# A selective-scan network on one core: the remainder of delta in a tile of its own, and delta * u on GpSimd

## The chip, the cores and the metric

The kernel runs on one core of one Trainium2 chip. The metric is the device time of one execution in microseconds. Three runs of the kernel before took 11978.79, 11985.35 and 12007.12 us; the median is 11985.35 us. One further execution was profiled.

Five engines appear below: TensorE (PE in the profile, its weight loads PEld), VectorE (DVE), ScalarE (ACT), GpSimd (POOL) and SyncE (SP), which issues all DMA transfers of this kernel from one queue. [...]

## The reference

The network has four layers on an input of 4 images of 64 x 64 pixels with 96 channels. Layers 0 and 1 are two-dimensional selective scans (a residual connection around each), layers 2 and 3 are attention and a feed-forward network with quantised weights. The change lies in layers 0 and 1. Cut to what matters:

```python
xz = einsum('bhwc,ec->bhwe', groupnorm(x), in_proj_w)       # 2 * E channels, E = 192
xx, z = split(xz, 2);  z = silu(z)
xc = silu(depthwise_conv3x3(xx) + conv_b)
xs = [xc by rows, xc by columns, both reversed]             # K = 4 directions, L = 4096 steps
dts, Bmat, Cmat = split(einsum('bkdl,kcd->bkcl', xs, x_proj_weight), [R, R + N])
delta = softplus(einsum('bkrl,kdr->bkdl', dts, dt_projs_weight) + dt_projs_bias)
# scan over L, with A = -exp(A_logs), N = 16 states per channel
h = exp(delta * A) * h + delta * B * u                      # u = xs
y = sum over n of h * C
out = out_proj(layernorm(sum of the 4 directions of (y + u * D)) * z)
```

Two quantities made from delta are needed for the scan: delta itself, for the decay exp(delta * A), and the product delta * u.

## The kernel before, in words

`run` goes through four phases: layer 0 with images 0 and 1, layer 0 with images 2 and 3, then layer 1 with the same two pairs. A phase has a preparation (`prepare`), a scan (`scan_phase`) and a finish (`finish`). The finish of one phase is interleaved with the preparation of the next: both are Python generators, `run` steps the finish a certain number of times for each step of the preparation (`ph.beside`). After the last finish `token_layers` computes layers 2 and 3.

**The preparation.** Statistics of the group norm come first, then the convolution of the first image (`convolve`), then the loop over images i, chunks c of 512 positions and directions k = 0 (by rows) and 1 (by columns), which calls `steps`. After each call of `steps` for the first image, two steps of the convolution of the second image are taken. So a preparation has three stretches: convolution alone; items of the first image with the convolution of the second ("convolution stage" below); and items of the second image alone ("tail"). In phases two to four the finish of the phase before runs beside all of them.

A convolution tap is one VectorE instruction on two SBUF operands, xp and xc (L268), eight of them per 512 positions, after a first one on ScalarE.

**`steps`.** One call handles direction k and its reverse, k + 2: two "items". TensorE makes dts, B and C of both (L291, tile c in PSUM); ScalarE adds a row of ones and copies to SBUF (L294, L295, tile xd); TensorE multiplies by the weights of delta (L308, tile d, two buffers in PSUM). Then for each of the two items:

- L316, ScalarE: delta = softplus(d), tile dl, 96 partitions x 1024 fp32 (two halves of 512 positions)
- L317, ScalarE: the first part, delta rounded to bf16, into parts[:, 0]
- L318, VectorE: du = delta * u, tile du_sb; u is a view of xc. For k = 0 its elements are adjacent (in either direction), for k = 1 they are 64 floats apart
- L319, VectorE: delta - first part, written over dl
- L321, SP: du goes to DRAM, twice (two copies, 384 KB each)
- L322, GpSimd: the second part, the rest rounded to bf16
- L323, VectorE: the third part, rest - second part, rounded to bf16
- L324, SP: the three parts go to DRAM (576 KB)

Delta is thus kept as three bf16 numbers whose sum is delta, so that the scan can spread it over partitions with one bf16 matrix product (L415). The tiles dl, parts and du_sb come from the pool "steps" with two buffers each: the third use of a tile waits until every reader of the first is done, du_sb and parts until their transfers have landed. There are 64 items in a phase and 256 in all.

**The order of the work.** In the preparation and the finish a list scheduler of the tile framework decides the order of the instructions on each engine from its own cost estimates, and sets the semaphore waits. In the scan the order is written out by hand.

**The scan.** A unit is 12 channels of one chunk for all 8 sequences and 16 states. Its tile h is filled with du by DMA (L399), multiplied by B on GpSimd (L409), scanned on VectorE (L426) with a decay that TensorE and ScalarE make (L415, L419), and contracted with C on TensorE (L444). The scan's tiles are allocated when the pools of the preparation have been released.

Of the kernel before, what the change touches and what calls it, by code (L numbers as in the profile page):

```python
# [9 lines left out]
F32 = mybir.dt.float32  # L10
# [4 lines left out]
ALU = mybir.AluOpType  # L15
# [7 lines left out]
C = 96  # L23
# [6 lines left out]
TC = 512  # L30
# [25 lines left out]
def scan_view(t, k, c):  # L56


    part, half = t.ap[0], t.ap[1]
    if k == 0:  # L60
        off, steps = TC * c, (HW, 1)
    elif k == 1:
        off, steps = ROWS * c, (1, HW)
    elif k == 2:
        off, steps = L - 1 - TC * c, (-HW, -1)
    else:
        off, steps = L - 1 - ROWS * c, (-1, -HW)
    return bass.AP(t.tensor, t.offset + off, [part, half, [steps[0], ROWS], [steps[1], HW]])


def view(t, off, *dims):

    return bass.AP(t.tensor, t.offset + off, [t.ap[0]] + [list(d) for d in dims])


def rows(t):

    if len(t.shape) == 2:
        return t.rearrange("p (r w) -> p r w", w=HW)
    return t.rearrange("p h (r w) -> p h r w", w=HW)  # L80
# [50 lines left out]
class Scans:  # L131
# [152 lines left out]
    def steps(self, ph, sp, xc, xp, dt_w, i, k, c):  # L284


        nc, cst = self.nc, self.cst
        u = scan_view(xc, k, c)
        ps = self.bank()
        for h in range(2):  # L290
            nc.tensor.matmul(rows(ps[:XD2]), xp[:, k, h], u[:, h], start=h == 0, stop=h == 1)  # L291
        xd = sp.tile([XD2, TC], F32, name="xd")

        nc.scalar.activation(xd[:XD], ps[:XD], AF.Identity, bias=cst.one_row[:XD])  # L294
        nc.scalar.activation(  # L295
            xd[64:], view(ps[64:XD2], TC - 1, (-1, TC)), AF.Identity, bias=cst.one_row[64:]
        )
        yield
        both = []
        for back in range(2):  # L300
            at = 64 * back
            g, cc = 2 * (k + 2 * back) + i, NC - 1 - c if back else c
            nc.sync.dma_start(ph.bc[cc][:, g], xd[at : at + 2 * NS])
            both.append((g, cc, scan_view(xc, k + 2 * back, cc), self.p_d.tile([C, 2, TC], F32, name="d")))
        for m in range(2):
            for back, (_, _, _, ps) in enumerate(both):
                part = slice(64 * back + 2 * NS, 64 * back + XD)
                nc.tensor.matmul(  # L308
                    ps[:, m], dt_w[part, k, m * C : (m + 1) * C], xd[part], start=True, stop=True
                )  # L310
        yield
        for g, cc, u, ps in both:
            delta = sp.tile([C, 2, TC], F32, name="dl")
            parts = sp.tile([C, NP16, 2, TC], BF16, name="parts")
            du = sp.tile([C, 2, TC], F32, name="du_sb")
            nc.scalar.activation(delta, ps, AF.Softplus)  # L316
            nc.scalar.copy(parts[:, 0], delta)  # L317
            nc.vector.tensor_tensor(rows(du), rows(delta), u, ALU.mult)  # L318
            nc.vector.tensor_tensor(delta, delta, parts[:, 0], ALU.subtract)  # L319
            for copy in range(2):  # L320
                nc.sync.dma_start(ph.du[cc][copy, g, :E].rearrange("(h e) t -> e h t", h=2), du)  # L321
            nc.gpsimd.tensor_copy(parts[:, 1], delta)  # L322
            nc.vector.tensor_tensor(parts[:, 2], delta, parts[:, 1], ALU.subtract)  # L323
            nc.sync.dma_start(  # L324
                ph.delta[cc][g].rearrange("n (h q) t -> q (n h) t", h=2),
                parts.rearrange("q n h t -> q (n h) t"),
            )
            yield
# [660 lines left out]
```

## Time and profile before

| what | value |
|---|---|
| median of three runs | 11985.35 us |
| the profiled execution | 11973.68 us, span 11971.9 us |
| granted TensorE clock, mean | 0.826 |
| VectorE busy | 10052.3 us (84%) |
| of it scans, L426 | 6345.7 + 868.3 us |
| of it products du, L318 | 416.2 us in 256 instructions |
| of it differences, L319 and L323 | 309.6 and 329.1 us |
| of it convolution taps, L268 | 713.8 us in 1024 instructions |
| GpSimd busy | 7465.3 us (62%) |
| of it h * B, L409 | 7021.1 us in 2048 instructions |
| of it casts, L322 | 416.1 us in 256 instructions |
| ScalarE busy | 7321.2 us (61%) |
| preparations (from the first statistics, or the last scan instruction, to the loads of the next scan) | 12 to 712, 2598 to 3450, 5320 to 6166, 8034 to 8886 us |
| first and last VectorE scan instruction of each scan | 737 to 2598, 3474 to 5320, 6192 to 8034, 8910 to 10768 us |

How to read it: "busy" is the time in which an engine has an instruction of this program under way. An instruction that is blocked after it began counts as busy for the whole time. A line of a group names source line, engine, operation, what it writes and reads with partitions x elements, the count, busy time and mean duration, then the idle time of the engine just before these instructions and what ended it. A line of the timeline gives start and duration in us, and in brackets the idle time of the engine before it and what ended that. A line of the waits names who waited for whom, the sum in us, how often, and the longest. A line of the busy times by stage gives, after the stretch and its length, the busy time and count of each engine, the granted TensorE clock, the busy share of the DMA engines, and their rate.

### The profile page before, as it was taken

What the parts mean: (1) busy time and instruction counts of PE and PEld (TensorE: products, weight loads), DVE (VectorE), ACT (ScalarE), POOL (GpSimd) and SP (SyncE); (2) the same over time, 40 slices, a digit from 0 to 9 for tenths busy, and PEclk for the clock granted to TensorE, in tenths of its full rate; (3) what the DMA queues carried; (4) which work ended last, traced back from release to release, by engine and by line L of the source; (5) the groups of instructions that cost most, each with busy time, mean ns of one, the idle gap of its engine ahead of it and who ended that gap; (6) DMA issues with size and microseconds to landing.
All of it is one profiled execution on the core that took longest, in us unless ns stands there. A gap on an engine that the chain in (4) does not pass through costs nothing.

```text
span 11971.9 us, 337755 instructions
## 1 busy us (share of the span) xinstructions
PE 8659.6 (72%) x144960; PEld 4597.6 (38%) x144960; DVE 10052.3 (84%) x10351; ACT 7321.2 (61%) x12109; POOL 7465.3 (62%) x2316
## 2 busy tenths in 40 slices
PE   3567777765767777765777777766677777777777
PEld 1124444442334444442334444433234444444333
DVE  6679999987769999987769999986769999993667
ACT  4556666655556666655556666654557666662556
POOL 0169999960149999970149999970139999990000
PEclk8579999986679989886679999986668999998887
DMA  3677777764677777765677777764677777763110
GB/s 98 185 244 254 255 252 252 252 206 138 197 231 255 254 256 257 257 216 143 193 226 256 258 257 252 258 219 136 199 221 258 255 254 250 254 232 125 18 21 11
DMA packets 952267, 2501.23 MB, mean 209 GB/s; under 512 B 324494, under 2 KB 607220, under 8 KB 819316
## 3 DMA queue, kind: packets, MB, share of 16 engines
q1 hardware_dynamic: 950772, 2479.63, 62.8%
q8 instruction: 1142, 18.71, 0.7%
q14 instruction: 353, 2.89, 0.1%
HBM read 1965.42 MB, written 513.80 MB: 207 GB/s over the span
## 4 chain that ended last, share of the span: by engine, by line
DMA 56%; PE 12%; DVE 11%; SPq 10%; ACT 5%; issue 4%; POOL 2%; POOLq 0%; DVEq 0%; ACTq 0%
DMA h<-du 52%; SPq L399 9%; DVE xc L268 4%; PE f L594 2%; POOL parts L322 2%; PE d L308 1%; PE c L291 1%; DVE parts L323 1%; DVE dl L319 1%; DVE du_sb L318 1%; DMA yk<-y 1%; PE c L251 1%; PE f L603 1%; PE f L674 1%; PE f L660 1%
## 5 line engine op out<-in xcount | busy, mean ns | idle before, releaser
L409 POOL TENSOR_TENSOR h<-h,b 128x1536 f32<-128x1536 f32 x2048 | 7021.1, 3461 | 533.5 <-DMA h<-du 191.9
L426 DVE TENSOR_TENSOR_SCAN h<-a,carry,h 128x512 f32<-128x512 f32 x5376 | 6345.7, 1259 | 174.6 <-POOL h L409 171.9
L419 ACT ACTIVATE a<-a,a_col 128x512 f32<-128x512 f32 x6144 | 4031.0, 664 | 1856.7 <-PE a L415 1830.9
L444 PEld LDWEIGHTS y<-h,cw 128*32 128x32 f32 x131072 | 2786.7, 128 | 3501.2 <-issue 1310.9
L444 PE MATMUL y<-h,cw 128*32 128x48 f32 x131072 | 3660.1, 266 | 527.3 <-DVE h L426 211.6
L415 PE MATMUL a<-dlt,rep 72*128 72x512 bf16 x6144 | 2526.8, 422 | 1302.3 <-DVE h L426 1212.9
L322 POOL CAST parts<-dl 96x1024 bf16<-96x1024 f32 x256 | 416.1, 1630 | 2793.0 <-DVE dl L319 2587.0
L456 ACT COPY d<-y 128x384 f32<-128x384 f32 x2048 | 979.8, 478 | 475.0 <-PE y L444 429.8
L426 DVE TENSOR_TENSOR_SCAN h<-a,h 128x512 f32<-128x512 f32 x768 | 868.3, 1200 | 165.5 <-ACT a L419 142.6
L415 PEld LDWEIGHTS <-rep 72*128 72x128 bf16 x6144 | 487.2, 98 | 829.0 <-issue 587.8
L308 PE MATMUL d<-xd,dt_w 7*96 7x512 f32 x1024 | 631.7, 905 | 237.5 <-ACT dl L316 149.6
L268 DVE SCALAR_TENSOR_TENSOR xc<-xp,conv_w,xc 96x512 f32<-96x512 f32 x1024 | 713.8, 756 | 54.8 <-ACT xc L266 38.9
L826 POOL MEMSET tn<- 1x4096 f32 x8 | 27.8, 3507 | 862.3 <-PE pa L846 515.1
L316 ACT ACTIVATE dl<-d 96x1024 f32<-96x1024 f32 x256 | 258.4, 1018 | 449.5 <-DVE parts L323 429.1
L318 DVE TENSOR_TENSOR du_sb<-dl,xc 96x1024 f32<-96x1024 f32 x256 | 416.2, 1633 | 116.7 <-ACT dl L316 73.0
L291 PE MATMUL c<-xc,x_proj 96*103 96x512 f32 x512 | 452.3, 1024 | 82.1 <-ACT xc L271 42.7
L594 PE MATMUL f<-yk,perm 128*128 128x384 f32 x1024 | 429.6, 564 | 95.4 <-DMA yk<-y 72.8
L251 PE MATMUL c<-rawi,in_w 96*96 96x512 f32 x256 | 206.0, 915 | 397.0 <-DVE rawi L247 312.1
L319 DVE TENSOR_TENSOR dl<-dl,parts 96x1024 f32<-96x1024 f32 x256 | 309.6, 1217 | 210.8 <-ACT parts L317 209.3
L323 DVE TENSOR_TENSOR parts<-dl,parts 96x1024 bf16<-96x1024 f32 x256 | 329.1, 1292 | 160.4 <-POOL parts L322 158.0
L308 PEld LDWEIGHTS d<-xd,dt_w 7*96 7x96 f32 x1024 | 171.8, 222 | 642.9 <-ACT dl L316 229.7
L361 ACT ACTIVATE cw<-c,gmask 128x256 f32<-128x256 f32 x512 | 286.0, 570 | 116.4 <-DMA dlt<-delta 58.1
(116 smaller groups left out, 5802.0 us busy)
## 6 DMA issues: line engine op xcount, KB each, us to landing
h<-du SPq DMA_DIRECT2D x1024, 768.0 KB
h<-du SPq DMA_DIRECT2D x2048, 384.0 KB
du<-du_sb SPq DMA_DIRECT2D x512, 384.0 KB
delta<-parts SPq DMA_DIRECT2D x256, 576.0 KB
dlt<-delta SPq DMA_DIRECT2D x512, 288.0 KB
y<-d SPq DMA_DIRECT2D x2048, 48.0 KB
yk<-y SPq DMA_DIRECT2D x256, 384.0 KB
ud<-xu SPq DMA_DIRECT2D x128, 192.0 KB
```

The source lines that it names most:

```text
L268: nc.vector.scalar_tensor_tensor(rows(acc), src, w, rows(acc), ALU.mult, ALU.add)
L291: nc.tensor.matmul(rows(ps[:XD2]), xp[:, k, h], u[:, h], start=h == 0, stop=h == 1)
L308: nc.tensor.matmul(ps[:, m], dt_w[part, k, m * C : (m + 1) * C], xd[part], start=True, stop=True)
L322: nc.gpsimd.tensor_copy(parts[:, 1], delta)
L399: self.nc.sync.dma_start(u.h[32 * first : 32 * (first + quarters), e : e + n].rearrange("p e t -> p (e t)"), source.rearrange("a g e t -> ...
L409: self.nc.gpsimd.tensor_tensor(h, h, b, ALU.mult)
L415: self.nc.tensor.matmul(u.a[n], self.cst.rep[:, h], u.dl[:, e], start=True, stop=True)
L419: self.nc.scalar.activation(u.a[n], u.a[n], AF.Exp, scale=u.ph.a_col[:, at : at + 1])
L426: self.nc.vector.tensor_tensor_scan(u.h[:, n], u.a.pop(n), u.h[:, n], 0.0 if u.c == 0 else u.ph.carry[:, at : at + 1], ALU.mult, ALU.add,)
L444: self.nc.tensor.matmul(view(u.y[32 * j : 32 * j + 32], l2 * EB, (8 * EB, 4), (1, EB)), u.ph.cw[u.c][:, l1, 8 * j + l2], view(u.h, 64 * l1 ...
L456: self.nc.scalar.copy(u.d[:, :, :, l1], u.y[:, : 32 * EB].rearrange("p (t h x) -> p t h x", t=4, h=2))
L594: nc.tensor.matmul(ps[:, : 4 * C].rearrange("p (w v e) -> p w v e", w=4, v=nv), cst.perm[:, k], view(t, off, (sw if k < 2 else -sw, 4), (1 ...
```

## The change

Two edits in `steps`. The product delta * u is issued on GpSimd instead of VectorE. The difference delta - first part no longer overwrites dl but goes to a new tile "rest", of the same size and from the same pool with two buffers; the second and the third part read it. All other lines are the same, but they stand one line lower from there on (L319 becomes L320, L322 becomes L323, L323 becomes L324, L409 becomes L410 and so on).

```diff
             du = sp.tile([C, 2, TC], F32, name="du_sb")
             nc.scalar.activation(delta, ps, AF.Softplus)
             nc.scalar.copy(parts[:, 0], delta)
-            nc.vector.tensor_tensor(rows(du), rows(delta), u, ALU.mult)
-            nc.vector.tensor_tensor(delta, delta, parts[:, 0], ALU.subtract)
+            nc.gpsimd.tensor_tensor(rows(du), rows(delta), u, ALU.mult)
+            rest = sp.tile([C, 2, TC], F32, name="rest")
+            nc.vector.tensor_tensor(rest, delta, parts[:, 0], ALU.subtract)
             for copy in range(2):
                 nc.sync.dma_start(ph.du[cc][copy, g, :E].rearrange("(h e) t -> e h t", h=2), du)
-            nc.gpsimd.tensor_copy(parts[:, 1], delta)
-            nc.vector.tensor_tensor(parts[:, 2], delta, parts[:, 1], ALU.subtract)
+            nc.gpsimd.tensor_copy(parts[:, 1], rest)
+            nc.vector.tensor_tensor(parts[:, 2], rest, parts[:, 1], ALU.subtract)
             nc.sync.dma_start(
                 ph.delta[cc][g].rearrange("n (h q) t -> q (n h) t", h=2),
                 parts.rearrange("q n h t -> q (n h) t"),
```

## The prediction

> **What bounds the kernel now.** I read the page first, then the busy times by stage, then waits and timeline of the stages that hold the edited lines. The page's busy times suggest a VectorE problem that GpSimd could share:
>
> ```profile
> PE 8659.6 (72%) x144960; PEld 4597.6 (38%) x144960; DVE 10052.3 (84%) x10351; ACT 7321.2 (61%) x12109; POOL 7465.3 (62%) x2316
> L409 POOL TENSOR_TENSOR h<-h,b 128x1536 f32<-128x1536 f32 x2048 | 7021.1, 3461 | 533.5 <-DMA h<-du 191.9
> L318 DVE TENSOR_TENSOR du_sb<-dl,xc 96x1024 f32<-96x1024 f32 x256 | 416.2, 1633 | 116.7 <-ACT dl L316 73.0
> ```
>
> But the 84% is mostly scans (L426), which the change doesn't touch. The edited lines run only in the four preparations (12 to 712, 2598 to 3450, 5320 to 6166 and 8034 to 8886 us), 64 items in each. I cut two preparations where the second convolution starts and where it ends:
>
> ```profile
> core 0: us, PE busy (x) PEld busy (x) DVE busy (x) ACT busy (x) POOL busy (x), PEclk, DMA share, GB/s
> ...
> 230.00:486.00 256.00, 134.45 (x192) 37.85 (x192) 205.65 (x223) 138.66 (x152) 45.82 (x27) 0.53 0.59 165
> 486.00:702.00 216.00, 159.40 (x174) 41.42 (x174) 127.67 (x99) 95.44 (x105) 53.93 (x33) 0.50 0.77 221
> ...
> 2875.00:3143.00 268.00, 180.22 (x363) 70.86 (x364) 222.59 (x283) 160.37 (x185) 46.27 (x26) 0.59 0.63 181
> 3143.00:3425.00 282.00, 234.99 (x617) 112.16 (x615) 176.47 (x233) 144.08 (x181) 43.96 (x31) 0.68 0.72 218
> ```
>
> In the convolution stages VectorE is the fullest engine (206 of 256 us, 223 of 268). In the first preparation's tail no engine is full: there a chain sets the pace, 6.4 us an item. In later tails TensorE is at 235 of 282, because the finish of the previous phase runs beside them.
>
> The timeline of the first tail shows the chain, and something more:
>
> ```profile
> 592.73 1.89 DVE L318 TENSOR_TENSOR du_sb<-dl,xc 96x1024 f32<-96x1024 f32 x1
> 592.92 2.60 POOL L322 CAST parts<-dl 96x1024 bf16<-96x1024 f32 x1 [4.81 <-DVE dl L319]
> 595.56 1.22 DVE L323 TENSOR_TENSOR parts<-dl,parts 96x1024 bf16<-96x1024 f32 x1 [0.94 <-POOL parts L322]
> 596.88 1.02 ACT L316 ACTIVATE dl<-d 96x1024 f32<-96x1024 f32 x1 [5.32 <-DVE parts L323]
> 597.80 1.03 ACT L317 CAST parts<-dl 96x1024 bf16<-96x1024 f32 x1
> 598.86 1.22 DVE L319 TENSOR_TENSOR dl<-dl,parts 96x1024 f32<-96x1024 f32 x1 [2.08 <-ACT parts L317]
> 600.20 1.04 POOL L322 CAST parts<-dl 96x1024 bf16<-96x1024 f32 x1 [4.68 <-DVE dl L319]
> ```
>
> The softplus waits for the third part (L323) of an item before it, since that is the last reader of the dl buffer; the first part (L317) is behind the softplus on ACT. That wait is what the new tile removes. Second, the same cast takes 1.04 us alone and 2.60 us when a product on VectorE began 0.19 us before it: it gets nothing done until the product ends. The convolution shows the lock in both directions:
>
> ```profile
> 258.90 2.20 DVE L268 SCALAR_TENSOR_TENSOR xc<-xp,conv_w,xc 96x512 f32<-96x512 f32 x2
> 259.11 1.44 POOL L322 CAST parts<-dl 96x1024 bf16<-96x1024 f32 x1 [21.49 <-DMA du<-du_sb]
> ```
>
> Two taps, usually 0.74 us each, take 2.20 us: the cast waits for the first, the second waits for the cast.
>
> [...] here L409 gives 3461/1536 = 2.25 ns a column[...] No GpSimd row before is strided, so this is unshown, but on VectorE L318 alternates between 1.22 us (k = 0, u contiguous) and 1.89 us (k = 1, u with a step of 64 floats).
>
> **The change, part by part.** An item is one direction of one chunk; 256 in all.
>
> (1) Product to GpSimd. VectorE loses 256 x 1.56 us = 400 us (mean of 1.22 and 1.89). GpSimd gains, for k = 0, 1024 x 2.25 ns = 2.31 us, and for k = 1 an estimate of 3.3 us[...]. Its bounds are 2.31 (stride is free) and 4.6 (doubled). Mean 2.8 us. Both engines' instructions still exclude each other, so what counts is their joint time, up 2.8 - 1.56 = 1.24 us an item.
>
> (2) Tile "rest". Softplus now waits for the product and the first difference, no longer for the third part. The tile has two buffers; nothing else is added. In the built order GpSimd mostly alternates product and cast, VectorE rest and third part; the cast is queued behind the next product, and the third part, its DMA on SP and the du DMAs behind that wait for the cast.
>
> (3) First tail, 33 items. New period: cast 1.00, product D at once behind it, third part 1.07 (blocked, it ends that long after its blocker: a third part recorded at 2.03 us began 0.08 us into a 1.03 us cast), rest 1.15, handing over 0.12: 3.34 + D. k = 0: 5.65, but TensorE needs 11.2 us a step of two items (3.74 + 2 x 3.72), 5.6 an item, so 5.7; k = 1: 6.64. Mean 6.17 against 6.39: 33 x -0.22 = -7 us. Softplus, first part and TensorE are hidden under the lock.
>
> (4) First convolution stage. Lock time before: 127 taps x 0.67 (ten back to back span 6.70) = 85, 28 products x 1.56 = 44, 27 x 2 differences x 1.15 = 62, 27 casts x 1.04 = 28: 219 of 256. After: products 78, sum 253. The 37 us that the lock was free are cover, but 17.5 of them are VectorE waiting for the input DMA of the convolution and 11.3 for its first tap on ACT, at a few places; products that wait there fill some 20 us. So 34 - 20 = +14 us. Ends: 0 (all filled) and 34.
>
> (5) Later convolution stages, three: 231 of 268 before, with seven 1.75 us products of the finish; plus 34. About 26 us of VectorE's work there has one SBUF input[...]: fill 22, so +12 each, +36. Later tails: TensorE and the finish's chain carry half; -3 each, -9.
>
> (6) The scheduler's new order has 294 instead of 273 activation table loads: 21 x 1.28 = 27 us on ACT, which is 54% busy (139 of 256). A quarter on the path: +6.
>
> Around the scans nothing moves: L409 is the only GpSimd work there and stays. Sum: -7 + 14 + 36 - 9 + 6 = +40 us on the profiled 11973.7 us, 12013.7; the median of the runs stands 11.7 above the profiled one, so 12,025 us.
>
> **Rivals.** *Chain cut wins (faster).* If the stride is free on GpSimd (D = 2.31 throughout), lock time in a convolution stage rises by 28 x 0.75 = 21 us, within its free 37, and the tails run at 5.8 us: 33 x -0.6 = -20, later ones -10 each; the freer softplus gives 5 in each convolution stage. Sum -20 - 30 - 20 = -70: 11,915 us. For it: ACT's waits on L323 (110 us in the first tail). Against it: VectorE itself pays 55% for the stride. It decides from D(k = 1) below some 2.6 us.
>
> *Nothing measurable.* Slack fills the convolution stages (+5 each), tails give it back: 11,985 us. For it: TensorE and DMA (0.77 busy in the tail) are close behind; against it: the lock has only 37 us free.
>
> *Dear stride.* D(k = 1) = 4.6: 0.65 us more an item on average, 256 x 0.65 = 166, of which 60% on the path: +100 on top of +40: 12,125 us. *No lock between a GpSimd product and VectorE's two-input work*, the change doing just what its words say: tails at 5.7, convolution stages 28 x 1.0 us shorter: -150; the stretched casts speak against it, and it goes into the faster cases.
>
> **How the numbers follow.** Slower by the shared lock (+40) 0.36, dear stride 0.14, nothing measurable 0.28, chain cut 0.18, no lock 0.04. A measurement of this kernel tells 0.3% (36 us) from no change. Faster 0.22; slower 0.48, since +40 lies close to the bound and some of its spread counts as same, made up by the dear case; same 0.30. Range 11,925 to 12,125, both signs; the likeliest case's own is 11,995 to 12,070.
>
> **What would show it.** Right: GpSimd products near 2.3 and 3.3 us when not blocked; taps, differences and third parts of 2 to 4 us where a product runs; the softplus no longer waiting for the third part; the first tail at 6.0 to 6.3 us an item; convolution stages 10 to 20 us longer; scans unchanged. Wrong: strided products under 2.6 us, taps that keep 0.74 us beside a product, or preparations that shrink; or a later scan start by a shift of SBUF addresses (the steps pool grows by 8 KB a partition), which I count at nothing because the units pool waits for the whole preparation anyway.

## The result, and the profile after

The changed kernel takes 12110.61 us (median of four runs, 12095.05 to 12127.45), beside 11984.52 us for the kernel before (four runs, 11978.79 to 12007.12): a ratio of 1.0100, with an interval of 1.0083 to 1.0116. That is 126 us slower. The forecast was 12,025 us in a range of 11,925 to 12,125: the direction and the main cause were right, the size was three times too small.

The profiled execution took 12127.45 us with a span of 12125.7 us, 153.8 us over the profiled one of before. The page's busy times and the groups of the edited lines (after names, shapes and count: busy us, mean ns, then idle time before them), after four groups of the page before that they are compared with:

```profile
L268 DVE SCALAR_TENSOR_TENSOR xc<-xp,conv_w,xc 96x512 f32<-96x512 f32 x1024 | 713.8, 756 | 54.8 <-ACT xc L266 38.9
...
L316 ACT ACTIVATE dl<-d 96x1024 f32<-96x1024 f32 x256 | 258.4, 1018 | 449.5 <-DVE parts L323 429.1
...
L319 DVE TENSOR_TENSOR dl<-dl,parts 96x1024 f32<-96x1024 f32 x256 | 309.6, 1217 | 210.8 <-ACT parts L317 209.3
L323 DVE TENSOR_TENSOR parts<-dl,parts 96x1024 bf16<-96x1024 f32 x256 | 329.1, 1292 | 160.4 <-POOL parts L322 158.0
```

and after:

```profile
PE 8618.3 (71%) x144960; PEld 4584.6 (38%) x144960; DVE 10184.3 (84%) x10095; ACT 7358.7 (61%) x12130; POOL 8208.3 (68%) x2572
...
L318 POOL TENSOR_TENSOR du_sb<-dl,xc 96x1024 f32<-96x1024 f32 x256 | 842.4, 3295 | 1320.5 <-ACT dl L316 973.4
L323 POOL CAST parts<-rest 96x1024 bf16<-96x1024 f32 x256 | 321.5, 1260 | 847.5 <-DVE rest L320 444.1
L268 DVE SCALAR_TENSOR_TENSOR xc<-xp,conv_w,xc 96x512 f32<-96x512 f32 x1024 | 848.8, 888 | 45.5 <-ACT xc L266 29.4
...
L324 DVE TENSOR_TENSOR parts<-rest,parts 96x1024 bf16<-96x1024 f32 x256 | 590.3, 2312 | 130.8 <-POOL parts L323 130.8
...
L320 DVE TENSOR_TENSOR rest<-dl,parts 96x1024 f32<-96x1024 f32 x256 | 373.7, 1463 | 242.5 <-ACT parts L317 241.8
...
L316 ACT ACTIVATE dl<-d 96x1024 f32<-96x1024 f32 x256 | 257.9, 1018 | 280.1 <-DVE rest L320 236.9
```

VectorE gave away 256 products, 416 us, and is busy 132 us longer than before. What it kept was stretched: the taps by 135.0 us (713.8 before), the third parts by 261.2 (329.1), the rests by 64.1 (309.6). These three outweigh the products by 44 us; tensor_scalar instructions and the finish's other VectorE work grew too (below). The ScalarE line shows the half of the change that works: the softplus no longer waits for the third part (429.1 us before), only for the rest (236.9).

The convolution stages of the first and the second preparation, cut at the same events as in the prediction (columns: stretch and length, then busy time and count of PE, PEld, DVE, ACT and POOL, granted clock, DMA share, GB/s):

```profile
237.00:511.00 274.00, 138.89 (x193) 38.44 (x192) 224.31 (x194) 147.40 (x158) 124.00 (x55) 0.53 0.55 155
...
2893.00:3176.00 283.00, 178.91 (x352) 68.57 (x352) 244.44 (x256) 163.55 (x188) 114.39 (x51) 0.57 0.58 165
```

In the first convolution stage VectorE has 29 instructions fewer (194 for 223) and is busy 19 us longer (224 for 206). The prediction's tails end at no common event (its second one stops 9 us before the last third part), so tails are compared by the table below alone.

For all that follows, a preparation is cut at its first tap, its 128th, its 129th and its last tap, and the first scan instruction. Lengths in us, read from the starts of these instructions in the trace:

| stage | before | after | difference |
|---|---|---|---|
| convolution alone, preparations 1 to 4 | 115.7, 123.2, 123.1, 122.8 | 120.0, 127.3, 127.4, 127.1 | +4.3, +4.1, +4.3, +4.3 |
| between the two images' taps | 53.4, 80.4, 80.3, 80.8 | 56.5, 76.2, 80.0, 77.6 | +3.1, -4.2, -0.3, -3.2 |
| convolution stage | 255.7, 268.0, 263.0, 266.1 | 273.7, 282.4, 282.0, 282.3 | +18.0, +14.4, +19.0, +16.2 |
| tail, to the first scan instruction | 251.7, 331.1, 333.8, 332.9 | 240.9, 351.1, 348.9, 345.9 | -10.8, +20.0, +15.1, +13.0 |
| whole preparations | 737.0, 874.7, 870.6, 875.0 | 751.6, 909.3, 909.4, 904.0 | +117.0 together |
| four scans | 7411.5 | 7444.4 | +32.9 |
| last finish and token layers | 1203.1 | 1207.0 | +3.9 |

The sum is the 153.8 us. The 33 us of the scans are most likely not the change's. The profiled execution of before is 10.8 us below the median of its runs and that of after 16.8 us above, which makes 28 of the 153.8 us. The experiments below, with either form of the edited lines, all have scans of 7446 to 7460 us, but beside them the kernel before takes 23 to 31 us more than here, so this alone would not decide. What the change costs lies in the preparations: 117 us, near the 126 us between the medians.

The timeline of the first tail shows the order of work that the prediction gave: cast, product at once behind it, third part blocked by the product, rest, then softplus and the next cast together (start us, length us, engine, line; in brackets the idle time before and its releaser):

```profile
601.32 1.03 POOL L323 CAST parts<-rest 96x1024 bf16<-96x1024 f32 x1 [2.34 <-DVE rest L320]
...
602.32 2.35 POOL L318 TENSOR_TENSOR du_sb<-dl,xc 96x1024 f32<-96x1024 f32 x1
602.39 3.36 DVE L324 TENSOR_TENSOR parts<-rest,parts 96x1024 bf16<-96x1024 f32 x1 [1.19 <-POOL parts L323]
...
605.67 1.21 DVE L320 TENSOR_TENSOR rest<-dl,parts 96x1024 f32<-96x1024 f32 x1
...
607.00 1.02 ACT L316 ACTIVATE dl<-d 96x1024 f32<-96x1024 f32 x1 [0.57 <-DVE rest L320]
607.00 1.03 POOL L323 CAST parts<-rest 96x1024 bf16<-96x1024 f32 x1 [2.34 <-DVE rest L320]
```

The third part takes 3.36 us instead of 1.22: it begins 0.07 us after the product and ends 1.08 us after the product's end. When the cast ends (602.35), GpSimd's product has begun (602.32); VectorE's third part follows at 602.39. So the product goes ahead of the third part: 27 of the 34 third parts of the first tail end 1.08 us after a product, and 16 of the 33 in each later tail. Products that nothing blocks take 2.34 us for k = 0 and 2.85 us for k = 1.

### The profile page after: what moved, and what is told of

It reads as the page before. It is cut to its first block, busy times and chain, and to the rows that moved or that the text cites. A ratio compares the mean times of both kernels' runs of the same rounds, so it can differ in the third digit from the quotient of the medians.

```text
span 12125.7 us, 337564 instructions
## 1 busy us (share of the span) xinstructions
PE 8618.3 (71%) x144960; PEld 4584.6 (38%) x144960; DVE 10184.3 (84%) x10095; ACT 7358.7 (61%) x12130; POOL 8208.3 (68%) x2572
## 5 line engine op out<-in xcount | busy, mean ns | idle before, releaser
L410 POOL TENSOR_TENSOR h<-h,b 128x1536 f32<-128x1536 f32 x2048 | 7021.2, 3461 | 565.8 <-DMA h<-du 222.3
L318 POOL TENSOR_TENSOR du_sb<-dl,xc 96x1024 f32<-96x1024 f32 x256 | 842.4, 3295 | 1320.5 <-ACT dl L316 973.4
L323 POOL CAST parts<-rest 96x1024 bf16<-96x1024 f32 x256 | 321.5, 1260 | 847.5 <-DVE rest L320 444.1
L268 DVE SCALAR_TENSOR_TENSOR xc<-xp,conv_w,xc 96x512 f32<-96x512 f32 x1024 | 848.8, 888 | 45.5 <-ACT xc L266 29.4
L308 PE MATMUL d<-xd,dt_w 7*96 7x512 f32 x1024 | 575.9, 915 | 274.1 <-ACT xd L294 207.2
L324 DVE TENSOR_TENSOR parts<-rest,parts 96x1024 bf16<-96x1024 f32 x256 | 590.3, 2312 | 130.8 <-POOL parts L323 130.8
L320 DVE TENSOR_TENSOR rest<-dl,parts 96x1024 f32<-96x1024 f32 x256 | 373.7, 1463 | 242.5 <-ACT parts L317 241.8
L316 ACT ACTIVATE dl<-d 96x1024 f32<-96x1024 f32 x256 | 257.9, 1018 | 280.1 <-DVE rest L320 236.9
L317 ACT CAST parts<-dl 96x1024 bf16<-96x1024 f32 x256 | 264.9, 1040 | 169.5 <-DMA delta<-parts 151.0
```

The costliest lines, as they stand in the source:

```text
L268: nc.vector.scalar_tensor_tensor(rows(acc), src, w, rows(acc), ALU.mult, ALU.add)
L308: nc.tensor.matmul(ps[:, m], dt_w[part, k, m * C : (m + 1) * C], xd[part], start=True, stop=True)
L318: nc.gpsimd.tensor_tensor(rows(du), rows(delta), u, ALU.mult)
L324: nc.vector.tensor_tensor(parts[:, 2], rest, parts[:, 1], ALU.subtract)
L410: self.nc.gpsimd.tensor_tensor(h, h, b, ALU.mult)
```

## The experiments

The theory: a product on GpSimd and VectorE's two-input work exclude each other, and the product is longer there than on VectorE; the tile alone is a gain. The rivals: the chain cut decides; nothing is lost to exclusion, and GpSimd's queue or the new order is at fault; the stride costs double. Ratios are to runs of the kernel before on the same chip, whose medians are 12013.1 us for the halves, the fills and the first image, 12007.84 us for the second image, the faster finish and the better version, and 12015.17 us for the pair with the finish apart.

### Each half of the change alone

Only the tile (from the kernel after):

```diff
-            nc.gpsimd.tensor_tensor(rows(du), rows(delta), u, ALU.mult)
+            nc.vector.tensor_tensor(rows(du), rows(delta), u, ALU.mult)
```

> Only the new tile: the product stays on VectorE. Theory of the lock (the loss comes from GpSimd's product and VectorE's two-input work excluding each other): the tile by itself helps, since the softplus no longer waits for the third part; first tail at 5.7 to 5.9 us an item, some 20 us shorter, later tails some 10 us each, convolution stages 0 to 5 us each: about 11,915 us, not above 11,985. Rival theory of the order (the new tile and the scheduler's new order, with 286 activation table loads instead of 273, cost the time, wherever the product runs): slower than before, 12,030 us or more.

Only the product (from the kernel before):

```diff
-            nc.vector.tensor_tensor(rows(du), rows(delta), u, ALU.mult)
+            nc.gpsimd.tensor_tensor(rows(du), rows(delta), u, ALU.mult)
```

> Only the product on GpSimd: the difference still overwrites dl. Lock: joint time as in the changed kernel, and in addition the overwriting difference has to wait for the product and the softplus for the third part, so one chain runs through softplus, product (2.3 or 2.85 us), difference, cast and third part, about 7.4 us an item in the first tail: slower than the changed kernel, 12,180 to 12,250 us. Order: the old tile brings back most of the old order (279 table loads), so faster than the changed kernel, at most 12,060 us.

Measured: the tile alone 11953.63 us, ratio 0.9941 (0.9928 to 0.9955); the product alone 12267.57 us, 1.0212 (1.0198 to 1.0226). The two halves have opposite signs. The tile saves 0.6%. The product costs 2.1% on the kernel before and 1.6% on top of the tile (1.0100 against 0.9941), so the tile doesn't pay for it; both together cost half of what the product costs alone. The product alone is slower than expected: its first tail runs at 8.1 us an item instead of 7.4. With the tile alone the first tail is 227.2 us, 24.5 shorter than before; the product on GpSimd brings it back to 240.9. The timeline of that tail with the tile alone:

```profile
571.38 1.22 DVE L320 TENSOR_TENSOR rest<-dl,parts 96x1024 f32<-96x1024 f32 x1 [0.65 <-ACT parts L317]
...
572.69 1.02 ACT L316 ACTIVATE dl<-d 96x1024 f32<-96x1024 f32 x1
572.72 1.04 POOL L323 CAST parts<-rest 96x1024 bf16<-96x1024 f32 x1 [3.24 <-DVE rest L320]
...
573.79 1.22 DVE L324 TENSOR_TENSOR parts<-rest,parts 96x1024 bf16<-96x1024 f32 x1 [1.19 <-POOL parts L323]
...
574.93 1.92 DVE L318 TENSOR_TENSOR du_sb<-dl,xc 96x1024 f32<-96x1024 f32 x1
```

Here the product comes behind the third part, and nothing in the chain is blocked: rest, cast and third part take 1.22, 1.04 and 1.22 us, as each does alone. The last items of this tail run at 5.6 us each (44.8 us for eight), which is TensorE's pace as the prediction worked it out: the chain is no longer what bounds it.

### The same GpSimd time without a reader

From the kernel after. du is filled with a constant instead, so this kernel leaves delta * u out. GpSimd gets three fills of 0.95 us and a copy of one element per partition, which keeps the wait for the softplus:

```diff
-            nc.gpsimd.tensor_tensor(rows(du), rows(delta), u, ALU.mult)
+            nc.gpsimd.tensor_copy(du[:, 1, TC - 1 :], delta[:, 1, TC - 1 :])
+            for _ in range(3):
+                nc.gpsimd.memset(du.rearrange("c h t -> c (h t)"), 0.001)
```

> The changed kernel with the product replaced on GpSimd by a copy of one column of dl (which keeps the wait for the softplus) and three fills of du_sb by a constant, together about as long as a product but reading nothing from SBUF. The product delta * u is left out of the computation. Lock: with nothing to exclude, the taps keep 0.74 us and the third parts 1.22 us beside the fills; the convolution stages fall below those of before (256 and 268 us) since VectorE is rid of 1.56 us an item, the loss of 126 us is gone and more: 11,850 to 11,950 us. Order, or GpSimd's queue (the cast stands behind a long instruction): the same 12,080 to 12,120 us as the changed kernel.

Measured: 11845.47 us, ratio 0.9862 (0.9849 to 0.9876). The page's groups:

```profile
L318 POOL COPY du_sb<-dl 96x1 f32<-96x1 f32 x256 | 201.6, 788 | 1261.9 <-ACT dl L316 1038.0
...
L268 DVE SCALAR_TENSOR_TENSOR xc<-xp,conv_w,xc 96x512 f32<-96x512 f32 x1024 | 746.7, 788 | 51.4 <-ACT xc L266 36.7
L320 POOL MEMSET du_sb<- 96x1024 f32 x768 | 730.1, 953 | 39.0
...
L322 DVE TENSOR_TENSOR rest<-dl,parts 96x1024 f32<-96x1024 f32 x256 | 310.6, 1216 | 304.9 <-ACT parts L317 304.3
```

(This kernel has two lines more: its L322 is the rest, L320 of after.) GpSimd is busy even longer than after (8299.1 us on the page, against 8208.3), in the same place in its queue, and the convolution stages shrink to 224 to 247 us: the taps fall from 888 to 788 ns (756 before) and the rests from 1463 to 1216 (1217 before). So it is neither GpSimd's time nor its queue that costs. What the fills lack is the product's reading of SBUF, and where a product reads, VectorE's two-input instructions stand still (a third part of 1.22 us took 3.36 in the first tail's timeline above).

### The product on GpSimd for one image only

From the kernel after, for the first image and then for the second:

```diff
-            nc.gpsimd.tensor_tensor(rows(du), rows(delta), u, ALU.mult)
+            (nc.gpsimd if i == 0 else nc.vector).tensor_tensor(rows(du), rows(delta), u, ALU.mult)
```

> The changed kernel, with the product on GpSimd for the items of the first image only (the convolution stage) and on VectorE for those of the second (the tail). Lock: convolution stages keep their loss of 14 to 19 us each, some 68 us together; the later tails lose their +13 to +20 us each and all tails get what the tile alone gives: about 12,000 us, between the tile alone and the changed kernel. Order: no difference by where the product runs, so about 12,100 us.

```diff
-            nc.gpsimd.tensor_tensor(rows(du), rows(delta), u, ALU.mult)
+            (nc.gpsimd if i == 1 else nc.vector).tensor_tensor(rows(du), rows(delta), u, ALU.mult)
```

> The new tile, with the product on GpSimd for the items of the second image (the tail) only. The order of the finish is the one of before (118 products by the fortieth item). Handed-on finish: convolution stages 255 to 261 us as with the tile alone, first tail near 241 us, later tails at 325 to 336 us; about 0.996 to 1.000 of before. Lock in the tail: later tails at 345 us or more, so 1.001 to 1.004 of before.

Measured: first image 12085.8 us, ratio 1.0061 (1.0043 to 1.0080); second image 12002.58 us, 0.9996 (0.9987 to 1.0005). By stage, in us:

| kernel | convolution alone, sum | convolution stages | first tail | later tails |
|---|---|---|---|---|
| before | 484.9 | 255.7, 268.0, 263.0, 266.1 | 251.7 | 331.1, 333.8, 332.9 |
| after | 501.7 | 273.7, 282.4, 282.0, 282.3 | 240.9 | 351.1, 348.9, 345.9 |
| tile alone | 485.7 | 255.2, 259.4, 258.0, 260.5 | 227.2 | 323.8, 331.9, 326.8 |
| first image on GpSimd | 502.2 | 274.7, 281.1, 282.5, 282.1 | 230.8 | 347.5, 345.2, 342.0 |
| second image on GpSimd | 484.7 | 258.2, 260.2, 260.3, 261.4 | 238.2 | 341.2, 340.5, 336.8 |

The convolution's loss comes whole with the first image's products and is absent without them, in convolution alone too. A product in the tail costs 11 us in the first tail and 9 to 17 in the later ones, over the tile alone. But the first image's products lengthen the *later* tails as well, by 13 to 24 us over the tile alone, although VectorE makes the products there. That was not expected: something is handed on from the convolution stage. About 8 us of it is the place of the cut: with the tile alone the softplus of the 33rd item starts 8.9 us before the last tap, with the first image's products on GpSimd 0.7 us before it, so that tail holds more of the items' work. Counted from that softplus, the later tails are 15.4, 5.2 and 7.1 us longer than with the tile alone. With the second image on GpSimd the later tails, 337 to 341 us, lie between what the two theories gave.

### What is handed on: two tries

In the kernel after, fewer of the finish's matrix products lie ahead of the last items. The first try was to step the finish faster, so that their order returns to that of before:

```diff
-            ph.beside = 0.6
+            ph.beside = 0.68
```

> The changed kernel with the share of the finish in the convolution stage raised from 0.6 to 0.68 steps of the finish per step of the preparation. In the changed kernel the scheduler puts 30 TensorE products of the finish behind the fortieth item of a phase that stood ahead of it before (88 instead of 118 by then); with 0.68 they are 118 again. Theory of the handed-on finish (later tails are 13 to 20 us longer because they receive finish work): later tails back at 325 to 338 us, convolution stages 0 to 8 us longer than the 282 us of the changed kernel; ratio to before about 1.007. Theory of the lock in the tail (the product on GpSimd itself makes the later tails longer): tails stay at 345 to 351 us, ratio 1.010 or above.

Measured: 12129.58 us, ratio 1.0099 (1.0084 to 1.0114), later tails 352.2, 349.1 and 349.4 us. That much did return: 544 of the finish's 960 matrix products start before the fortieth softplus of a phase, as before, against 488 in the kernel after. Nothing came back: the tails stay as long. Here the finish ends 14 us before the last third part (0.6 us behind it in the kernel after), so the finish's own end isn't what holds the tail up.

The second try takes the finish away from beside the preparation, in both kernels, and issues it afterwards:

```diff
                         due += phases[p].beside
-                        while due >= 1.0:
-                            next(end, None)
-                            due -= 1.0
+                        pass
```

> The kernel before, with the finish of a phase no longer stepped beside the next preparation but issued after it. It is the base for the run beside it. Both theories: slower than before by the part of the finish that the preparation had covered, some +150 to +500 us; without the finish the later tails should stand near the first one (251 us) instead of 333, and the later convolution stages near 256 instead of 266.

> The changed kernel, with the finish issued after the preparation in the same way. What is compared is the difference to the same form of the kernel before. Theory A, the later tails lose by the work of the finish that stands beside them (its VectorE work waits for GpSimd's products too, and delays the chain): without it every tail gains as the first one does (-11 us), convolution alone loses 4 and the convolution stage 18, so the difference is 4 x (+11) = some +44 us, +0.3 to +0.5 per cent, and each tail is 5 to 15 us shorter than in the same form of the kernel before. Theory B, the later tails lose by themselves (their own items are slower with the product on GpSimd, whatever stands beside): the difference stays at +100 to +130 us, about +0.9 to +1.1 per cent, and the later tails are 13 to 20 us longer than in the same form of the kernel before.

Measured: 12613.92 us for the form of before (ratio 1.0496, 1.0481 to 1.0512), 12677.9 us for that of after (1.0550, 1.0533 to 1.0568). Both are slow, but what counts is their difference: 64 us or 0.5%, where the kernels themselves differ by 126. The tails now include the whole finish; each is shorter with the change:

| tail, us | 1 | 2 | 3 | 4 |
|---|---|---|---|---|
| before, finish apart | 253.6 | 585.5 | 581.3 | 581.7 |
| after, finish apart | 243.3 | 569.5 | 568.8 | 570.1 |

The convolution stages lose 18 to 20 us each, as in the first preparation (253.5 to 255.4 before, 273.2 to 274.2 after). All four preparations together grow by 57 us instead of 117. So the tails lose nothing by themselves: they lose when the finish runs beside them, and half of the change's cost hangs on that. The finish takes its matrix products, its ScalarE and VectorE work and its transfers with it, so the pair doesn't tell which of them matters.

One candidate shows in the trace. VectorE's groups of the finish, in the whole execution, before:

```profile
L643 DVE TENSOR_SCALAR s<-s,mv_f,r_f 128x192 f32<-128x192 f32 x256 | 84.5, 394 | 0.9
...
L667 DVE TENSOR_TENSOR s<-s,z 128x1536 f32<-128x1536 f32 x32 | 56.0, 1749 | 48.5 <-ACT z L663 48.5
```

and after:

```profile
L644 DVE TENSOR_SCALAR s<-s,mv_f,r_f 128x192 f32<-128x192 f32 x256 | 99.2, 451 | 0.7
...
L668 DVE TENSOR_TENSOR s<-s,z 128x1536 f32<-128x1536 f32 x32 | 71.5, 2235 | 85.8 <-ACT z L664 85.8
```

The finish's own VectorE instructions wait for GpSimd's products: L644 in the tails (mean of the whole execution 452 ns also with the second image alone on GpSimd, 403 with the first), L668 in the convolution stages (2235 ns with the first image alone, 1753 with the second). Summed over the three later preparations, the finish's VectorE work (L630 to L700) grows from 172.3 to 187.7 us between the first tap and the last, and from 192.1 to 213.0 us in the tails. That is 5 and 7 us a preparation, less than the 13 to 20 us by which the tails grow. And in the tails it is neither enough nor needed to lengthen them: with the fills this work takes 213.1 us as well, and the later tails last 328.7 to 331.6 us; with the first image alone it takes 192.1 us, as before, and they last 342 to 348. How the tails' loss comes about was not settled.

### A better version

The tile alone, with the second part made on ScalarE, so that GpSimd does nothing in the preparations (edited from the kernel after, with the product back on VectorE as above):

```diff
-            nc.gpsimd.tensor_copy(parts[:, 1], rest)
+            nc.scalar.copy(parts[:, 1], rest)
```

> A version that may beat both: the tile alone, and the second part's cast on ScalarE instead of GpSimd, so that GpSimd has nothing in the preparation and VectorE is never excluded. Lock: VectorE's blocked time goes (27 casts of 1.04 us in a convolution stage), convolution stages 5 to 15 us below the tile alone's 255 to 260; in the tail ScalarE gets 1.04 us more an item (to 4.8 us of 5.8) and the chain keeps its length, so tails unchanged or up to 15 us longer: 0.985 to 0.998 of before. If ScalarE's order is what binds: above 1.000.

Measured: 11863.38 us, ratio 0.9874 (0.9856 to 0.9892). It leaves nothing out and is faster than both kernels: 1.3% under before, 2.2% under after (0.9874 / 1.0100). The convolution stages are 237.3, 243.3, 250.2 and 246.7 us, the later tails 326.1, 323.5 and 324.2. The first preparation's convolution stage, and the first 200 us of its tail:

```profile
225.00:462.00 237.00, 136.78 (x192) 38.26 (x192) 193.59 (x223) 171.15 (x184) 0.00 (x0) 0.54 0.63 178
462.00:662.00 200.00, 136.42 (x174) 34.17 (x174) 128.27 (x99) 127.78 (x136) 0.00 (x0) 0.50 0.86 246
```

VectorE still makes all products (223 instructions) and is busy 194 us here, 12 less than before: GpSimd has no cast there (0.00, x0) for it to wait for. ScalarE pays 32 us more than before (171 for 139) and has room for it.

## Why the prediction was right in direction and too small

**Step (1), the product's price.** k = 0: 2.31 us predicted, 2.34 measured. k = 1: 3.3 taken, my estimate (no strided product ran on GpSimd before), 2.85 measured; the stride costs 22%, not 43%. The mean is 2.60 us instead of 2.8, so the joint time rises by 1.04 us an item and not 1.24. This term was too high. The rival "dear stride" (4.6) falls.

**Step (2), the waits.** Right: the softplus waits for the rest, and cast, product, third part and rest follow each other as written down.

**Step (3), the first tail, -7 us.** Measured -10.8. The period for k = 0 was put at 5.7 us; 601.32 to 607.00 is 5.68. With 2.85 in place of 3.3 the step's own formula gives 6.19 for k = 1 and a mean of 5.95; eight items took 47.3 to 47.7 us after the first eight, 5.9 to 6.0 each. The mechanism and the formula hold. For 33 items the formula then gives -15 us; counted from the softplus of the 33rd item the tail shrinks by 13.4 us, counted from the last tap by the 10.8.

**Steps (4) and (5), the convolution stages, +14 and +12 each: +50.** Measured +18.0, +14.4, +19.0, +16.2: +67.6. With the cheaper product the sum of lock time should have been smaller, so the cover was overrated; that is argued from the sum, not shown by a run. One reason can be read from the runs: the 26 us of one-input work that I let run beside GpSimd, an estimate that no run had shown. Part of it is tensor_scalar, which did not keep its time: L644 (L643 before) goes from 394 to 451 ns, and the group L247, which normalises the convolution's input, from 539 to 621, while the finish's BATCH_NORM_STATS2 (L634, L633 before) keeps 339. How many of the missing us this explains was not measured. Products that fill idle time at waits are the other part of the cover, and no run separates them.

**Convolution alone, counted at nothing.** It costs 4.3 us each time, 17 in all, and only with products of the first image on GpSimd. The timeline after, where the first items meet that stretch:

```profile
148.81 24.59 DVE L268 SCALAR_TENSOR_TENSOR xc<-xp,conv_w,xc 96x512 f32<-96x512 f32 x37
149.41 30.07 POOL L318 TENSOR_TENSOR du_sb<-dl,xc 96x1024 f32<-96x1024 f32 x2 [148.96 <-ACT dl L316]
```

VectorE's order is the same as before here: 37 taps, then the stretch's last two taps among the first items' differences. These two took 0.74 us each before; now one takes 2.82 us and the other starts at 180.5 instead of 176.3, since each waits for products. I had counted the items' work from the convolution stage on.

**Step (5), later tails, -3 each: the step that failed.** Measured +20.0, +15.1 and +13.0, 57 us from the forecast and the larger part of the error. I had TensorE and the finish's chain "carry half" of these tails, as cover for the product. The finish is not cover: beside it the later tails lose 13 to 20 us, and with the finish apart all four tails gain 10 to 16, as step (3) had it for the first. What the step left out is that the product and the finish could hold each other up; by what path they do stays open. The runs speak against two: the finish's VectorE work in the tails (as long with the fills, where the tails are 16 to 22 us shorter than after) and the finish's own end (14 us earlier when it is stepped faster, with tails as long).

**Step (6), table loads, +6.** ScalarE has 21 instructions more (12130 for 12109) and is 37.5 us longer busy. No run separates the loads. With the finish stepped faster there are 309 instead of 294, and the ratio is the same (1.0099 and 1.0100), which speaks for less than +6; open.

**Around the scans nothing.** Right, with the note on their 33 us above.

**The rivals.** "Chain cut wins" is what the tile alone does (0.9941). It was to decide for the whole change below a k = 1 product of some 2.6 us; that took 2.85, and the product on GpSimd costs 1.6% on top. "No lock" falls with the fills: the lock is what they take away. "Nothing measurable" falls by the interval.

**The sum.** +40 predicted; +117 in the preparations: first tail -11 (-7), convolution stages +68 (+50), convolution alone +17 (0), later tails +48 (-9), between the taps -5 (0), and table loads, which are inside these (+6). Errors of both signs meet in it: the product was priced too high, the cover too high as well.

**Where luck came in.** The likeliest case had a range of its own, 11,995 to 12,070, and the result lies 41 us above it. It lies within the whole range because that reached up to the dear stride's 12,125 us, and that case did not come true.

## What to carry to other kernels

Before work is moved from VectorE to GpSimd, count GpSimd's instructions that read SBUF and VectorE's two-input ones as one sum of time, since here they excluded each other (a cast of 1.04 us took 2.60, a third part of 1.22 us took 3.36), and VectorE's tensor_scalar ones with them, since here they grew (L644 from 394 to 451 ns); if the work is longer on GpSimd, as here by 1.04 us an item, the move lengthens that sum, and idle time on GpSimd (busy 46 of the 256 us of the first convolution stage before) was no cover for it. What runs beside a stage (here the finish) is not cover until a run shows it: taken apart from it, the tails gained; beside it they lost. Of an edit with two halves, time each alone: here one gained 0.6% and the other hid it.

## What the runs showed of the hardware that was not expected

- VectorE kept GpSimd out for a whole run of back-to-back two-input instructions, not for one. The product begun at 149.41 us (timeline above; the line holds two) ended at 176.7, after the 37 taps and the rest behind them. The first product of the first phase took 27.3 us, and the second of each later phase 26.2 us, instead of 2.34.
- GpSimd's product of two fp32 operands of 96 x 1024 took 2.34 us with both adjacent and 2.85 us with one of them at a step of 256 bytes: 22% more. On VectorE the same step cost 55% (1.22 to 1.89 us).
- Beside GpSimd's fills, which write only, VectorE's differences kept their time (1216 ns) and the taps nearly (788 ns, 756 before), but tensor_scalar did not. Its group in the second preparation's later part, in the run with the fills (32 instructions; 437 ns each in the later tail of before):

```profile
L646 DVE TENSOR_SCALAR s<-s,mv_f,r_f 128x192 f32<-128x192 f32 x32 | 18.3, 625 | 0.1
```

- A blocked third part needed less than its full time once it was let go: one that began 0.07 us into a product ended 1.08 us after it, against 1.22 us alone.
